# Corner sums of a bilinear gather: from wide SBUF multiplies to a PSUM accumulator, tap by tap, with new planner costs

## The chip, the cores and the metric

One NeuronCore of a Trainium2 chip runs the whole program. The metric is device time in microseconds of one execution, as the median of several; lower is better. The engines named below are PE (TensorE, matrix multiplies), DVE (VectorE), ACT (ScalarE), POOL (GpSimd) and SP (SyncE, which issues most DMAs). Each runs its own instructions in the order in which they were issued, and they wait for each other on semaphores.

## The reference, cut to what matters

Four layers are applied to each of four samples of shape 96 x 128 x 128: a two-direction selective scan (layer 0), a convolution mixed with Fourier transforms (layer 1), a modulated deformable convolution (layer 2), and a cosine transform with a 16-state scan (layer 3). Each is a residual branch behind a group normalisation. The change is in layer 2. Its core:

```python
offset = _conv(x, offset_w, offset_b)
mask = jax.nn.sigmoid(_conv(x, mask_w, mask_b))
for k in range(K * K):
    i, j = (k // K, k % K)
    py = base_y[None, :, None] + i * DIL + offset[:, 2 * k]
    px = base_x[None, None, :] + j * DIL + offset[:, 2 * k + 1]
    # v00, v01, v10, v11: the pixels around (py, px), zero outside
    samp = ((1 - wy_) * (1 - wx_) * v00 + (1 - wy_) * wx_ * v01
            + wy_ * (1 - wx_) * v10 + wy_ * wx_ * v11) * mask[:, k][:, None]
    out = out + jnp.einsum('bchw,oc->bohw', samp, weight[:, :, i, j])
return out + bias[None, :, None, None]
```

So each output pixel has nine taps, each tap four corners, and each corner 96 channels with one weight per pixel, tap and corner (the mask is multiplied into it beforehand).

## The kernel before, in words

**Stages.** For each sample there is a `front` (layer 0, layer 1, and the offsets, indices and corner weights of layer 2), a `back` (the gather of layer 2, and the head and first transform of layer 3), `layer3` (its scans) and an `inverse` transform. The program runs: the front of sample 0; then, for each sample b, one mixed stage with the back of b, the inverse of b-1 and the front of b+1, followed by layer3 of b; at the end the inverse of the last sample. The last mixed stage has no front.

**The planner.** In the prologue and in mixed stages, `Program` (from line 235) records every engine operation of two lanes, the back in lane 0, inverse and front in lane 1, and then issues them in an order that a list scheduler works out: it keeps a clock for each engine, gives each operation a duration from `cost` (line 351) and, between engines, `LATENCY` (line 243), and takes next, on the engine that can start soonest, the operation with the lowest key among those that can start within `LATENCY`. The key is an operation's place in its own lane, as a share of that lane's length, so both lanes advance in proportion. The order that comes out is fixed in the program; on the chip, each engine follows it whatever the real durations are. Since the recorder issues all operations, the profile shows line 65 for all of them, and tiles' names tell them apart. `layer3` uses another class, `Order`, with costs of its own.

**The gather** (`gather`, line 1270). A DRAM tensor `quad_d` holds, for each pixel, the 4 x 96 channels of a 2 x 2 neighbourhood. For each of 128 image rows and nine taps, POOL issues an indirect DMA that fetches 384 numbers for each of 128 pixels into `l_g` (three row buffers of 128 x 9 x 384). The loop at line 1344 runs over rows and taps: while row r is fetched, row r-1 is weighed, row r-2 is turned, and once in four rows a group of four is finished.

- `weigh` (line 1297), in three parts of three taps each: DVE multiplies 128 x 1152 numbers of `l_g` in place with their weights `l_v` (one weight spread over 96 channels), adds the second half of each tap's corners to the first (128 x 576), and adds the last two corners into `l_sm` (128 x 288). All three are on SBUF.
- `turn` (line 1311), in two parts: PE transposes `l_sm` in pieces of 128 columns into the PSUM tile `l_pt` (four in the first part, three in the second), and ACT copies them to `l_sT` on SBUF.
- `finish` (line 1328), in four parts: PE multiplies seven chunks of `l_sT`, for four rows at once, with the layer's weights into the PSUM tile `l_pc`; in the last part DVE adds bias and residual (`l_x`) and takes statistics of it.

The row buffer of `l_g` is free for a new row when `weigh` is done with it. `l_pt` and `l_pc` share one PSUM tag with two buffers. PSUM has eight banks; layer 0's own tags hold six of them (`a` three, `b` one, `c` two), the gather's two.

Of the kernel before, what the change touches and what calls it, by code (L numbers as in the profile page):

```python
# [45 lines left out]
def lanes(ap, n):  # L46

    return ap.unsqueeze(2).to_broadcast([ap.shape[0], ap.shape[1], n])
# [188 lines left out]
class Program:  # L237
# [4 lines left out]

    LATENCY = 0.12
    SPAN = (1.0, 1.0)
# [106 lines left out]
    def cost(self, engine, name, out, ins):  # L351

        if engine == "SP":
            v = next(v for v in [out, *ins] if isinstance(v, View) and v.tile.kind == "SBUF")
            return 0.1, 1.4e-5 * v.at[0].size * (v.rows[1] - v.rows[0])
        n = out.at[0].size
        if name == "indirect_dma_start":
            return 1.25, 0.68
        if engine == "PE":
            return (0.28 if name == "transpose" else 0.06 + 0.8 * n / CH), None  # L360
        if engine == "ACT":
            return 0.12 + 0.001 * n, None
        if engine == "POOL":
            return 0.1 + 0.0023 * n, None
        if name == "tensor_tensor_scan":
            return 0.1 + 0.0022 * n, None
        fast = name in ("tensor_copy", "tensor_scalar", "memset") and all(
            v.tile.kind == "SBUF" for v in [out, *ins]
        )
        return 0.09 + n / (1900 if fast else 960), None  # L370

# [122 lines left out]
class Net:  # L494
# [106 lines left out]
    def layer0(self, xin, T):  # L601
# [3 lines left out]
        with self.program.pool(name="l0w", bufs=1) as wp, self.program.pool(name="l0p", bufs=1, space=PSUM) as ps:  # L605
# [32 lines left out]
            for k in range(2):  # L638
                pw = ps.tile([128, CH], F32, name="l0_pw", tag="a", bufs=3)
                nc.tensor.matmul(out=pw[:C, :C], lhsT=xpd[:, k, :], rhs=dtT[:, k, :], start=True, stop=True)  # L640
                yield
                nc.vector.tensor_copy(wd[:, k, :], pw[:C, :C])
                for n in range(2):
                    nc.vector.tensor_copy(
                        wbc[:, 2 * k + n, :], xpT[:, k, R6 + n : R6 + n + 1].to_broadcast([C, C])
                    )
                yield
            scale, shift, _ = yield from self.group_norm(st0, ps, "a", 3)

            with self.program.pool(name="l0a", bufs=3) as wa:  # L650

                def block(i):
# [5 lines left out]
                    for g in range(4):  # L658
                        s = slice(BR * i * W + g * CH, BR * i * W + (g + 1) * CH)
                        pc = ps.tile([C, CH], F32, name="l0_pc", tag="a", bufs=3)  # L660
                        yield from self.conv9(pc, wc, xb, i, g)
# [15 lines left out]
            with self.program.pool(name="l0b", bufs=3) as wb:  # L677
                edges = [None, None]

                def scan(k, n):  # L680
# [60 lines left out]

                    pm = ps.tile([C, CH], F32, name="l0_pm", tag="a", bufs=3)
                    nc.tensor.matmul(out=pm, lhsT=center[:, 1, :], rhs=uc, start=True, stop=False)
# [7 lines left out]
                    yield  # L751
                    pv = ps.tile([C, CH], F32, name="cn_v", tag="a", bufs=3)
                    nc.tensor.matmul(out=pv, lhsT=self.cavg, rhs=sq, start=True, stop=True)
# [9 lines left out]
                    yield  # L763
                    po = ps.tile([C, CH], F32, name="l0_po", tag="a", bufs=3)
                    nc.tensor.matmul(out=po, lhsT=woT, rhs=ct, start=True, stop=True)
# [504 lines left out]
    def gather(self, T, wp, wb, ps):  # L1270
# [26 lines left out]
        def weigh(row, m):  # L1297
            g3 = gts[row][:, 3 * m : 3 * m + 3]
            if m == 0:
                sms[row] = wb.tile([128, 9, C], F32, name="l2_sm", tag="sm")  # L1300
            w4 = work[row // 4].w4[:, 36 * (row % 4) + 12 * m : 36 * (row % 4) + 12 * m + 12]
            gq = g3.rearrange("p k (q c) -> p (k q) c", c=C)
            nc.vector.tensor_tensor(gq, gq, lanes(w4, C), ALU.mult)
            nc.vector.tensor_tensor(
                g3[:, :, 0 : 2 * C], g3[:, :, 0 : 2 * C], g3[:, :, 2 * C : 4 * C], ALU.add
            )
            nc.vector.tensor_tensor(
                sms[row][:, 3 * m : 3 * m + 3], g3[:, :, 0:C], g3[:, :, C : 2 * C], ALU.add
            )

        def turn(row, m):
            w = work[row // 4]
            if row % 4 == 0 and m == 0:
                w.sT = wb.tile([128, KC, 4, W], F32, name="l2_sT", tag="sT")
            flat = sms[row].rearrange("p k c -> p (k c)")
            pt = ps.tile([128, 4, W], F32, name="l2_pt2", tag="t")
            k = 4 - m
            for j in range(k):
                at = (4 * m + j) * 128
                n = min(128, 9 * C - at)  # L1320
                nc.tensor.transpose(pt[:n, j, :], flat[:, at : at + n], self.ident)
            if m:
                nc.scalar.copy(w.sT[:, 4:6, row % 4, :], pt[:, 0:2])
                nc.scalar.copy(w.sT[:C, 6, row % 4, :], pt[:C, 2])
            else:
                nc.scalar.copy(w.sT[:, 0:4, row % 4, :], pt)

# [16 lines left out]
        for row in range(H + 3):  # L1344
            if row % 4 == 2 and row // 4 + 1 < H // 4:
                fetch(row // 4 + 1)
            for k in range(9):
                if row < H:
# [8 lines left out]
                    )  # L1357
                if k in (2, 4, 6) and 0 <= row - 1 < H:
                    weigh(row - 1, k // 2 - 1)
                if k in (1, 5) and 0 <= row - 2 < H:  # L1360
# [827 lines left out]
```

## Time and profile before

| | us |
|---|---|
| median of 7 runs | 18461.31 |
| lowest and highest of them | 18437.08, 18539.92 |
| the profiled execution | 18512.09 |
| its span | 18510.3 |
| DVE busy in the span | 13137.2 |
| POOL busy | 11661.8 |
| PE busy | 14440.1 |
| ACT busy | 8165.8 |

How to read the profile's lines: a group of instructions is named by its engine, its operation, what it writes and reads (`out<-in`, without buffer numbers), its shapes and its count; after the bar stand its busy time in us and the mean of one in ns, then the time for which the engine was idle just before such instructions, with what ended most of that. "issue" is idle time in which the engine waited for nothing that the profile shows, "remote" such that was ended by something the profile can't name. In a table of windows, each row is one stretch of the span, with every engine's busy time and count, then the clock granted to PE as a share of full speed, the DMA engines' share and GB/s. In a timeline a row is one or more instructions that follow each other, with start, length, and in brackets the engine's idle time before it.

### The profile page before, as it was taken

To read this page: it belongs to the slowest core of one execution; us is meant where nothing else is said; L and a number is where in the kernel's file an instruction comes from. 1 tells how busy PE (TensorE), PEld (TensorE's weight loads), DVE (VectorE), ACT (ScalarE), POOL (GpSimd) and SP (SyncE) were. 2 spreads that over 40 slices of the span, in tenths; PEclk is the share of its full clock that TensorE was granted. 3 is DMA by queue.
4 is the path that set the end of the run, shared out by engine and by line. 5 is a ranking of instruction groups with operands and counts; after the bars stand their busy time and mean duration, and the time that the engine had idled before them with its cause. 6 is when DMAs were issued, how large, how long until landed. Compare 5 with 4: busy or idle time off the path is not lost. (4 is left out here: it accounts for less than half of the span.)

```text
span 18510.3 us, 150202 instructions
## 1 busy us (share of the span) xinstructions
PE 14440.1 (78%) x41152; PEld 6545.3 (35%) x41152; DVE 13137.2 (71%) x17010; ACT 8165.8 (44%) x15519; POOL 11661.8 (63%) x9556
## 2 busy tenths in 40 slices
PE   7896877888988787888999587787899733248988
PEld 2363323543333322633333332454333311113334
DVE  1625586568998577667999658666899755557997
ACT  2612252126776143215777235213777500016776
POOL 0103686536887587553888668562788766656887
PEclk9897887989999888888999788798999955569999
DMA  3525557550001657553000555665000244440001
GB/s 82 159 78 160 166 163 210 162 171 27 9 7 43 180 163 208 161 163 108 9 7 8 150 159 164 201 172 171 11 7 9 70 143 139 137 124 23 9 7 48
DMA packets 1189374, 1939.48 MB, mean 105 GB/s; under 512 B 191985, under 2 KB 711601, under 8 KB 1169457
## 3 DMA queue, kind: packets, MB, share of 16 engines
q1 hardware_dynamic: 893616, 1023.60, 19.0%
q0 software_dynamic: 294912, 906.26, 17.0%
q8 instruction: 329, 5.39, 0.1%
q14 instruction: 517, 4.23, 0.1%
HBM read 1473.67 MB, written 455.61 MB: 104 GB/s over the span
## 5 line engine op out<-in xcount | busy, mean ns | idle before, releaser
L65 POOL DMA_INDIRECT l_g<-quad_d,l_i x4608 | 5450.5, 1183 | 3768.5 <-DVE l_sm L65 1443.8
L65 POOL TENSOR_TENSOR l_hc<-l_h,l_cs 128x512 f32<-128x512 f32 x3072 | 3854.6, 1274 | 848.3 <-PE l_py L65 264.4
L65 DVE TENSOR_TENSOR_SCAN l_h<-l_dA,l_carry,l_dB 128x512 f32<-128x512 f32 x3072 | 3916.3, 1275 | 166.4 <-ACT l_carry L65 74.5
L65 DVE TENSOR_TENSOR l_g<-l_g,l_v 128x1152 f32<-128x1152 f32 x1536 | 2085.2, 1358 | 911.0 <-DMA l_g<-quad_d,l_i 822.3
L65 ACT ACTIVATE l_dA<-l_dl,l_al 128x512 f32<-128x512 f32 x3072 | 2183.0, 722 | 802.4 <-DVE l_h L65 801.6
L65 ACT COPY l_sT<-l_pt 128x512 f32<-128x512 f32 (+2 forms) x1536 | 575.6, 407 | 4198.0 <-PE l_pt L65 2314.2
L65 PE MATMUL l_pt<-ident,l_sm 128*128 128x128 f32 (+1 forms) x3584 | 884.2, 340 | 1950.6 <-issue 726.2
L65 PE MATMUL l_py<-l_hc,ident 128*128 128x512 f32 x4608 | 2389.6, 608 | 18.4 <-POOL l_hc L65 10.1
L65 DVE TENSOR_TENSOR l_dB<-l_du,l_pB 128x512 f32<-128x512 f32 x3072 | 2135.8, 695 | 319.7 <-POOL l_du L65 26.7
L65 PE MATMUL l_pB<-l_bc,pick 128*128 128x512 f32 x3072 | 1781.2, 580 | 554.5 <-DVE l_dB L65 521.8
L65 ACT COPY l_cs<-l_pC 128x512 f32<-128x512 f32 x3072 | 1785.2, 581 | 630.0 <-PE l_pC L65 540.4
L65 PE MATMUL l_pC<-l_bc,pick 128*128 128x512 f32 x3072 | 1549.7, 504 | 118.8 <-ACT l_cs L65 108.4
L65 PEld LDWEIGHTS l_pt<-ident,l_sm 128*128 128x128 f32 (+1 forms) x3584 | 510.5, 167 | 2773.2 <-issue 1840.8
L65 PEld LDWEIGHTS l_pB<-l_bc,pick 128*128 128x128 f32 x3072 | 582.3, 190 | 2198.7 <-DVE l_dB L65 2104.6
L65 DVE TENSOR_TENSOR l_g<-l_g 128x576 f32<-128x576 f32 x1536 | 1165.2, 759 | 36.1
L65 PE MATMUL l_p<-rows,l_c 96*96 96x508 f32 (+2 forms) x2304 | 1076.0, 610 | 33.8 <-DMA rows<-cat_d 17.2
L65 PE MATMUL l_pc<-rows,l_wc 96*96 96x508 f32 (+2 forms) x2304 | 1083.6, 608 | 10.6 <-issue 5.6
L65 PE MATMUL l_pu<-l_xq,l_wc 96*64 96x512 f32 (+1 forms) x2048 | 1078.6, 616 | 13.6 <-ACT l_xq L65 13.6
L65 PE MATMUL l_pc<-l_sT,l_wk 128*96 128x512 f32 (+1 forms) x1792 | 986.7, 670 | 62.6 <-ACT l_sT L65 36.6
L65 PEld LDWEIGHTS l_py<-l_hc,ident 128*128 128x128 f32 x4608 | 882.7, 193 | 379.2 <-issue 173.6
L65 POOL TENSOR_TENSOR l_hc<-l_hc 128x512 f32<-128x512 f32 x768 | 977.9, 1273 | 55.2
L65 DVE TENSOR_TENSOR l_sm<-l_g 128x288 f32<-128x288 f32 x1536 | 699.7, 472 | 353.4 <-remote 221.2
(252 smaller groups left out, 20861.9 us busy)
## 6 DMA issues: line engine op xcount, KB each, us to landing
quad_d<-l_qt SPq DMA_DIRECT2D x124, 768.0 KB
x<-l_x SPq DMA_DIRECT2D x384, 192.0 KB
l_g<-quad_d,l_i POOLq DMA_INDIRECT x4608
mix<-l_mx SPq DMA_DIRECT2D x256, 256.0 KB
sp_in<-mix SPq DMA_DIRECT2D x256, 256.0 KB
l_uc<-u_d SPq DMA_DIRECT2D x256, 192.0 KB
l_x<-x SPq DMA_DIRECT2D x256, 192.0 KB
l_xs<-x SPq DMA_DIRECT2D x116, 256.0 KB
```

The costliest lines, as they stand in the source:

```text
L65: ins = op(*args, **kw).ins
```

## The change

It has three parts.

1. `weigh` runs in two parts instead of three, over taps 0 to 4 and 5 to 8, when row r's taps 2 and 5 are fetched (2, 4 and 6 before). Each part takes a PSUM tile `l_acc` of 128 x 5 x 96 (one bank, one buffer). For each tap ACT writes the first corner times its weight into `l_acc`, with the weight as a scale by pointer; then DVE adds the second and third corner to it, one multiply-add of 128 x 96 for each tap and corner, and the fourth corner's multiply-add writes to `l_sm`. `l_g` is only read.
2. `turn` transposes three pieces in its first part and four in its second (four and three before), since the first part of `weigh` makes five taps, which is 480 columns.
3. To make room for `l_acc`, layer 0's PSUM tag `a` has two buffers instead of three. The planner's costs are changed: `LATENCY` 0.2 instead of 0.12, and other durations by kind of operation.

```diff
-    LATENCY = 0.12
+    LATENCY = 0.2
...
         if engine == "PE":
-            return (0.28 if name == "transpose" else 0.06 + 0.8 * n / CH), None
+            return (0.2 if name == "transpose" else 0.06 + 0.83 * n / CH), None
         if engine == "ACT":
-            return 0.12 + 0.001 * n, None
+            return 0.12 + (0.0009 if name == "copy" else 0.0011) * n, None
         if engine == "POOL":
+            return 0.2 + 0.0023 * n, None
+        if name == "tensor_tensor_scan":
             return 0.1 + 0.0023 * n, None
-        if name == "tensor_tensor_scan":
-            return 0.1 + 0.0022 * n, None
...
-        return 0.09 + n / (1900 if fast else 960), None
+        return (0.1 if n < 200 else 0.14) + n / (1900 if fast else 960), None
...
-                        pc = ps.tile([C, CH], F32, name="l0_pc", tag="a", bufs=3)
+                        pc = ps.tile([C, CH], F32, name="l0_pc", tag="a", bufs=2)
...
         def weigh(row, m):
-            g3 = gts[row][:, 3 * m : 3 * m + 3]
             if m == 0:
                 sms[row] = wb.tile([128, 9, C], F32, name="l2_sm", tag="sm")
-            w4 = work[row // 4].w4[:, 36 * (row % 4) + 12 * m : 36 * (row % 4) + 12 * m + 12]
-            gq = g3.rearrange("p k (q c) -> p (k q) c", c=C)
-            nc.vector.tensor_tensor(gq, gq, lanes(w4, C), ALU.mult)
-            nc.vector.tensor_tensor(
-                g3[:, :, 0 : 2 * C], g3[:, :, 0 : 2 * C], g3[:, :, 2 * C : 4 * C], ALU.add
-            )
-            nc.vector.tensor_tensor(
-                sms[row][:, 3 * m : 3 * m + 3], g3[:, :, 0:C], g3[:, :, C : 2 * C], ALU.add
-            )
+            acc = ps.tile([128, 5, C], F32, name="l2_acc", tag="acc", bufs=1)
+            w4 = work[row // 4].w4
+            taps = range(5 * m, 5 + 4 * m)
+            for q in range(4):
+                for k in taps:
+                    at = 36 * (row % 4) + 4 * k + q
+                    g, w = gts[row][:, k, q * C : (q + 1) * C], w4[:, at : at + 1]
+                    a_ = acc[:, k - 5 * m, :]
+                    if q == 0:
+                        nc.scalar.activation(a_, g, AF.Copy, scale=w)
+                    else:
+                        o = sms[row][:, k, :] if q == 3 else a_
+                        nc.vector.scalar_tensor_tensor(o, g, w, a_, ALU.mult, ALU.add)
...
-            k = 4 - m
+            k = 3 + m
             for j in range(k):
-                at = (4 * m + j) * 128
+                at = (3 * m + j) * 128
...
             if m:
-                nc.scalar.copy(w.sT[:, 4:6, row % 4, :], pt[:, 0:2])
-                nc.scalar.copy(w.sT[:C, 6, row % 4, :], pt[:C, 2])
+                nc.scalar.copy(w.sT[:, 3:6, row % 4, :], pt[:, 0:3])
+                nc.scalar.copy(w.sT[:C, 6, row % 4, :], pt[:C, 3])
             else:
-                nc.scalar.copy(w.sT[:, 0:4, row % 4, :], pt)
+                nc.scalar.copy(w.sT[:, 0:3, row % 4, :], pt[:, 0:3])
...
-                if k in (2, 4, 6) and 0 <= row - 1 < H:
-                    weigh(row - 1, k // 2 - 1)
+                if k in (2, 5) and 0 <= row - 1 < H:
+                    weigh(row - 1, k // 5)
```

The other four PSUM tiles of layer 0's tag `a`, and the call of the group normalisation that uses it, change from three to two buffers in the same way.

More of the change, by code (lines that the diff above doesn't have):

```diff
@@ L638, in layer0 @@
             for k in range(2):
-                pw = ps.tile([128, CH], F32, name="l0_pw", tag="a", bufs=3)
+                pw = ps.tile([128, CH], F32, name="l0_pw", tag="a", bufs=2)
                 nc.tensor.matmul(out=pw[:C, :C], lhsT=xpd[:, k, :], rhs=dtT[:, k, :], start=True, stop=True)
@@ L647, in layer0 @@
                 yield
-            scale, shift, _ = yield from self.group_norm(st0, ps, "a", 3)
+            scale, shift, _ = yield from self.group_norm(st0, ps, "a", 2)
             with self.program.pool(name="l0a", bufs=3) as wa:
@@ L739, in scan @@
                     yield
-                    pm = ps.tile([C, CH], F32, name="l0_pm", tag="a", bufs=3)
+                    pm = ps.tile([C, CH], F32, name="l0_pm", tag="a", bufs=2)
                     nc.tensor.matmul(out=pm, lhsT=center[:, 1, :], rhs=uc, start=True, stop=False)
@@ L751, in scan @@
                     yield
-                    pv = ps.tile([C, CH], F32, name="cn_v", tag="a", bufs=3)
+                    pv = ps.tile([C, CH], F32, name="cn_v", tag="a", bufs=2)
                     nc.tensor.matmul(out=pv, lhsT=self.cavg, rhs=sq, start=True, stop=True)
@@ L763, in scan @@
                     yield
-                    po = ps.tile([C, CH], F32, name="l0_po", tag="a", bufs=3)
+                    po = ps.tile([C, CH], F32, name="l0_po", tag="a", bufs=2)
                     nc.tensor.matmul(out=po, lhsT=woT, rhs=ct, start=True, stop=True)
```

## The prediction

> **What bounds the kernel now.** I read the page first, then the busy times stage by stage, then one stretch of the stage in which the gather runs without a front beside it, then the groups of single stages.
>
> ```profile
> span 18510.3 us, 150202 instructions
> ...
> L65 POOL DMA_INDIRECT l_g<-quad_d,l_i x4608 | 5450.5, 1183 | 3768.5 <-DVE l_sm L65 1443.8
> ...
> L65 DVE TENSOR_TENSOR l_g<-l_g,l_v 128x1152 f32<-128x1152 f32 x1536 | 2085.2, 1358 | 911.0 <-DMA l_g<-quad_d,l_i 822.3
> ```
>
> ```profile
> core 0: us, PE busy (x) PEld busy (x) DVE busy (x) ACT busy (x) POOL busy (x), PEclk, DMA share, GB/s
> 0.00:1530.00 1530.00, 1304.00 (x3998) 628.51 (x3999) 557.26 (x920) 490.13 (x991) 91.64 (x68) 0.94 0.38 109
> ...
> 5950.00:8570.00 2620.00, 2072.84 (x6547) 1007.77 (x6546) 1714.46 (x2498) 744.10 (x1600) 1557.09 (x1248) 0.85 0.61 178
> ...
> 14700.00:16700.00 2000.00, 684.87 (x2206) 344.65 (x2204) 1130.49 (x1403) 210.61 (x499) 1218.12 (x1185) 0.61 0.49 142
> ```
>
> The span falls into a front alone (1530 us), three mixed stages (2760, 2620 and 2680 us: gather of one sample beside the front of the next), a last gather stage with only the short inverse beside it (2000 us), and four layer3 stages (1660, 1760, 1690 and 1811 us), which the change doesn't touch. In a mixed stage no engine is full: PE 2073/2620 = 79%, DVE 65%, POOL 59%. What one is late for changes within the stage: in 6500 to 7000 us (the scans of layer 0) POOL is busy 405 us and idle 54 us more between gathers while PE's clock is down to 0.84; in 7500 to 8000 us PE is busy 444 of 500. The last gather stage is DVE's: 814 gathers in 15000 to 16250 us are 90.4 rows, so a row takes 13.8 us, though POOL can issue one in 9 x 1.25 = 11.3 us. There the instructions stand so:
>
> ```profile
> start us, us, engine line op out<-in xcount [idle before <-releaser]
> ...
> 15501.64 0.76 DVE L65 TENSOR_TENSOR l_g<-l_g 128x576 f32<-128x576 f32 x1
> 15502.43 0.46 DVE L65 TENSOR_TENSOR l_sm<-l_g 128x288 f32<-128x288 f32 x1
> 15502.73 0.98 POOL L65 DMA_INDIRECT l_g<-quad_d,l_i  x1 [0.30 <-issue]
> 15502.81 1.35 DVE L65 TENSOR_TENSOR l_g<-l_g,l_v 128x1152 f32<-128x1152 f32 x1
> 15503.01 0.47 PEld L65 LDWEIGHTS l_pt<-ident,l_sm 128*128 128x128 f32 x3 [2.32 <-issue]
> 15503.04 0.87 PE L65 MATMUL l_pt<-ident,l_sm 128*128 128x128 f32 x3 [1.95 <-DVE l_sm L65]
> 15503.94 0.53 ACT L65 COPY l_sT<-l_pt 128x256 f32<-128x256 f32 x2 [2.24 <-issue]
> 15504.02 0.96 POOL L65 DMA_INDIRECT l_g<-quad_d,l_i  x1 [0.30 <-issue]
> 15504.19 0.76 DVE L65 TENSOR_TENSOR l_g<-l_g 128x576 f32<-128x576 f32 x1
> ```
>
> To be seen here: a Vector instruction that needs the one before it starts 0.03 us after its end (15502.81 + 1.35 to 15504.19); one that doesn't starts 0.08 us before that end (15502.43 + 0.46 to 15502.81). Vector goes on with the next taps while PE and ACT turn the last ones.
>
> **Vector's part, step by step.** Removed per row: three times (1358 + 759 + 472 ns) = 7.8 us. Added: 27 multiply-adds of 96 elements. Their price comes from these rows of the last gather stage and of the whole:
>
> ```profile
> L65 DVE SCALAR_TENSOR_TENSOR l_x<-l_pc,l_bk,l_x 96x512 f32<-96x512 f32 x32 | 23.9, 746 | 445.1 <-remote 181.0 <-PE l_pc L65 132.6 <-issue 131.5
> ```
>
> This is the same operation with a scalar by pointer and one PSUM operand, 746 ns at 512 elements. 1152 and 576 elements give a slope of (1358 - 759)/576 = 1.04 ns, so 96 elements cost 746 - 416 x 1.04 = 313 ns. The other end is the multiply-add on SBUF alone that makes l_idx, 301 ns at 144: 301 - 48 x 1.04 = 251 ns. No row writes PSUM from Vector; I take 313, whose operands are nearest. In the built order all of the second and third products, and the first of the fourth ones, wait for the instruction just before them, although it is another tap; only the other fourth products are free. So a batch of n taps takes 2n x (d + 0.03) + (n - 1)(d - 0.08) + d: at 0.313 this is 4.7 us for five taps and 3.8 for four, 8.4 a row (+0.6 over today); at 0.251 it is 6.8 (-1.0).
>
> The Trainium skill speaks against the cut: "VectorE: DVE Perf Modes", "Rules for kernel authors", advises for chained operations to keep their count low rather than to fuse. Its formula (N + 151)/0.96 GHz gives 257 ns for 96 elements, an estimate by which a row would be 6.9 us; the row of 746 ns lies 55 ns above what the same formula gives for 512, so the trace's price is dearer.
>
> **ACT's part and the hand-over.** Nine products of 96 elements a row. Dearest: l_dA (scale by pointer, SBUF to SBUF) 722 ns at 512, with the slope of ACT's copies (586 - 372)/256 = 0.84 ns: 722 - 416 x 0.84 = 373 ns. Cheapest: the copy of 96x128, 264 ns, less 32 x 0.84: 237. In the built order each waits for the one before (+0.03), and the first multiply-add waits for the last product of its batch. There is one accumulator buffer, so the first product waits until Vector has finished the batch before. ACT and Vector therefore take turns: neither end of today's chain has this wait. In the last stage ACT also has the copies of the turned sums between the second and third product, and these wait for PE's transposes of the batch just finished: 1.05 us from l_sm's end (15502.89) to the copy (15503.94), the copies 0.37 + 0.26 or about 0.5, then three or two more products. With 0.40 a product: 1.05 + 0.63 + 1.2 = 2.9 and 1.05 + 0.5 + 0.8 = 2.35, so 5.2 us a row in which Vector stands; with 0.27 it is 4.6.
>
> **The sum by stage.** Last gather stage, dear end: 8.4 + 5.2 + four hand-overs of 0.1 = 14.0 us, plus l_x and its statistics (746 + 690 ns every four rows, 0.4), plus today's idle time before l_x unchanged (445.1/128 = 3.5): 17.9 a row, against 13.8 today, x 128 = +530 us. Cheap end: 6.8 + 4.6 + 0.4 + 0.4 + 1 (the wait before l_x cut to that) = 13.2, x 128 = -80 us. I take the middle, +220. Mixed stages: Vector's own work +0.6 x 128 = +80 us. In the built order half of a stage's 256 batches follow the one before on Vector with nothing between; 128 x about 1.8 us of products (five of 0.40 or four) = 230 us is the most that it then stands. Both shown: +310. Against it: POOL's gather takes 1234 ns in 5950 to 8570 us, 1018 in the last stage, and 0.95 us where Vector is idle, so what replaces the two-operand multiplies can return up to (1234 - 1018) ns x 1152 = 250 us. Since PE, not Vector, is nearest to full, I take a third of the loss and a fifth of the gain: +50 each, +150 for three. ACT has the room for 9 x 0.4 x 128 = 460 us a stage (744 of 2620 busy). Front alone: layer 0's PSUM tag loses one of three buffers. What hides this is that a group of nine tap matmuls of about 0.6 us (5.4 us) covers a 0.68 us ACT read; in the 300 us of scans, with three chained tiles per step, the cover is thin: between 0 and 30 us, taken as 15, with the new costs' reordering (below nothing is possible too: -30). Sum: 220 + 150 + 15 = +385 on 18,510 (the execution ran 18,512 us, the span nearly all of it); the median of the runs is 18,461, 50 below, so I forecast 18,850 us. Its own range: 18,600 to 19,300.
>
> The Trainium skill bears on the gain, too: "SBUF — State Buffer" states that Vector and GpSimd share a port pair that a Vector instruction with two SBUF inputs holds for its whole length. The 0.95 against 1234 ns agrees; by the rule alone all of the gather's stretching by the weighing would go.
>
> **The rivals.** *POOL set free (ends faster).* The new multiply-adds have one SBUF tensor instead of two. If POOL sets the pace of the scan phase (405 + 54 of 500 us there, gathers of 1480 ns), then the gathers' shortening shows: half of 250 us less 30 for Vector = about -95 in each mixed stage, and the cheap end -80 in the last: 18,461 - 365 = about 18,100. For it: DVE's waits for the gather's landing, 287 us in one mixed stage. Against: Vector's and ACT's turns are longer than the span saved. It decides once a chained multiply-add is below about 0.27 us. *Turns everywhere.* The dear ends hold in all stages: 3 x 310 + 530 = +1460, 19,920 us. For it: ACT's in-order queue blocks front evacuations behind a product that waits for Vector, with only two PSUM buffers. Against: 906 us of Vector's time in such a stage is idle now. *Nothing moves:* l_x's wait and PE set both kinds of stage, and the new work fills idle time: 18,461.
>
> **How the numbers follow.** Forecast 0.46, turns everywhere 0.12, nothing 0.08, POOL free 0.34. A measurement of this kernel tells 0.3% (55 us) from no change: slower 0.58, same 0.08, faster 0.34. The range must reach into POOL's case and part of the turns': 18,200 to 19,450 leaves about 1 in 10 at each end.
>
> **What would show it.** Right: l_acc multiply-adds near 313 ns, rows of the last gather stage at 15 us or more, Vector's idle time before l_acc ended by ACT, the last stage longer than 2000 us by some 220, the layer3 stages as before. Wrong: multiply-adds at 250 ns or less; gathers near 1000 ns in the mixed stages and these below 2600 us; the front alone moving by over 50 us.

## The result, and the profile after

The changed kernel took 18603.59 us (median of 14 runs, 18564.81 to 18622.49) beside 18523.83 us of the kernel before (35 runs, 18429.07 to 18582.09): a ratio of 1.0052, 95% interval 1.0038 to 1.0067. It is slower by half a per cent, by 80 us; 18,850 us had been forecast, 389 more than the 18,461 us of the first seven runs of the kernel before.

From the page of the changed kernel, the span and the groups of the new weighing (busy time, mean ns of one, then the idle time before them and what ended most of it):

```profile
span 18584.4 us, 171591 instructions
...
L65 POOL DMA_INDIRECT l_g<-quad_d,l_i x4608 | 4499.0, 976 | 4705.6 <-ACT l_acc L65 2156.9
L65 DVE SCALAR_TENSOR_TENSOR l_acc<-l_g,l_v,l_acc 128x96 f32<-128x96 f32 x9216 | 2965.6, 322 | 1989.2 <-ACT l_acc L65 1272.0
...
L65 ACT ACTIVATE l_acc<-l_g,l_v 128x96 f32<-128x96 f32 x4608 | 1583.1, 344 | 3302.4 <-DVE l_sm L65 2132.8
...
L65 DVE SCALAR_TENSOR_TENSOR l_sm<-l_g,l_v,l_acc 128x96 f32<-128x96 f32 x4608 | 1141.3, 308 | 286.4 <-PE l_pt L65 98.2
```

POOL's gathers fell from 1183 to 976 ns. The price is in the two waits: Vector stood 1272 us for ACT's products, and ACT stood 2133 us for the end of Vector's batch. Each of the two waits for the other over one accumulator.

The span is cut at the scans of layer3, which last about 1660 us in each of its four stages in both traces. What lies between, in us (the first stretch is the front alone with the first mixed stage):

| stretch | before | after | difference |
|---|---|---|---|
| start to first layer3 scan | 4273 | 4269 | -4 |
| second mixed stage | 2714 | 2768 | +54 |
| third mixed stage | 2710 | 2754 | +44 |
| last gather stage | 2091 | 2076 | -15 |

The sum, +79 us, is near the difference of the medians (79.8 us) and of the two spans (74 us). The second and third mixed stages lost about the 50 us each that had been forecast. The first stretch, for which +65 stood in the sum (15 for the front, 50 for its mixed stage), did not lose: up to the first gather it became 28 us shorter (1653 to 1625 us), and behind it 24 us longer (2620 to 2644). The last gather stage, for which +220 had been forecast, did not lose at all.

One turn in the last gather stage of the changed kernel, from its timeline (start, length, in brackets the idle time of the engine):

```profile
15501.38 0.99 DVE L65 SCALAR_TENSOR_TENSOR l_sm<-l_g,l_v,l_acc 128x96 f32<-128x96 f32 x4
15501.84 1.09 PE L65 MATMUL l_pt<-ident,l_sm 128*128 128x128 f32 x4 [4.80 <-DVE l_sm L65]
15502.41 0.72 ACT L65 ACTIVATE l_acc<-l_g,l_v 128x96 f32<-128x96 f32 x2 [3.93 <-DMA l_g<-quad_d,l_i]
...
15503.07 0.62 ACT L65 COPY l_sT<-l_pt 128x384 f32<-128x384 f32 x2
15503.59 1.10 ACT L65 ACTIVATE l_acc<-l_g,l_v 128x96 f32<-128x96 f32 x3
15504.72 3.55 DVE L65 SCALAR_TENSOR_TENSOR l_acc<-l_g,l_v,l_acc 128x96 f32<-128x96 f32 x10 [2.35 <-ACT l_acc L65]
15508.38 1.21 DVE L65 SCALAR_TENSOR_TENSOR l_sm<-l_g,l_v,l_acc 128x96 f32<-128x96 f32 x5
```

Vector ends a batch at 15502.37. ACT then makes two products, copies the turned sums, makes three more, and only when the fifth has ended (15504.69) does Vector begin: 2.35 us of standing before a batch of five taps, and 1.82 before one of four. A row is 8.6 us of Vector's work and 4.2 us of this. In the same stage, the groups of 15000 to 16250 us have this line:

```profile
L65 DVE SCALAR_TENSOR_TENSOR l_x<-l_pc,l_bk,l_x 96x512 f32<-96x512 f32 x23 | 17.2, 747 | 76.4 <-PE l_pc L65 58.1 <-remote 10.9 <-issue 7.4
```

Before `l_x` Vector waited 76.4/23 = 3.3 us for a group of four rows, against 445.1/32 = 13.9 in the kernel before. That is 2.7 us a row less. A second wait of the kernel before is gone as well, the one before `l_sm`. Here is its group in 14700 to 16700 us before, then in 15000 to 16250 us after:

```profile
L65 DVE TENSOR_TENSOR l_sm<-l_g 128x288 f32<-128x288 f32 x384 | 175.9, 458 | 294.9 <-remote 210.5 <-issue 67.9
```

```profile
L65 DVE SCALAR_TENSOR_TENSOR l_sm<-l_g,l_v,l_acc 128x96 f32<-128x96 f32 x833 | 203.9, 310 | 11.1 <-DVE l_acc L65 1.4
```

That is 294.9/128 = 2.3 us a row against 0.1. Together the two waits are 4.9 us a row shorter. That covers the 4.2 us of the turns and what Vector's own work grew by, so the stage did not lose.

### The profile page after: what moved, and what is told of

It reads as the page before. It is cut to its first block, busy times and chain, and to the rows that moved or that the text cites. A ratio compares the mean times of both kernels' runs of the same rounds, so it can differ in the third digit from the quotient of the medians.

```text
span 18584.4 us, 171591 instructions
## 1 busy us (share of the span) xinstructions
PE 14454.7 (78%) x41152; PEld 6583.7 (35%) x41152; DVE 13408.2 (72%) x26226; ACT 9537.5 (51%) x20127; POOL 10677.0 (57%) x9556
## 5 line engine op out<-in xcount | busy, mean ns | idle before, releaser
L65 POOL DMA_INDIRECT l_g<-quad_d,l_i x4608 | 4499.0, 976 | 4705.6 <-ACT l_acc L65 2156.9
L65 DVE SCALAR_TENSOR_TENSOR l_acc<-l_g,l_v,l_acc 128x96 f32<-128x96 f32 x9216 | 2965.6, 322 | 1989.2 <-ACT l_acc L65 1272.0
L65 ACT ACTIVATE l_acc<-l_g,l_v 128x96 f32<-128x96 f32 x4608 | 1583.1, 344 | 3302.4 <-DVE l_sm L65 2132.8
L65 DVE SCALAR_TENSOR_TENSOR l_sm<-l_g,l_v,l_acc 128x96 f32<-128x96 f32 x4608 | 1141.3, 308 | 286.4 <-PE l_pt L65 98.2
L65 PE MATMUL l_pc<-rows,l_wc 96*96 96x508 f32 (+2 forms) x2304 | 1080.1, 611 | 13.8 <-DVE rows L65 12.2
L65 PE MATMUL l_p<-rows,l_c 96*96 96x508 f32 (+2 forms) x2304 | 1054.8, 601 | 27.1 <-DMA rows<-cat_d 13.9
L65 PEld LDWEIGHTS l_pC<-l_bc,pick 128*128 128x128 f32 x3072 | 583.4, 190 | 994.5 <-ACT l_cs L65 671.8
```

The costliest lines, as they stand in the source:

```text
L65: ins = op(*args, **kw).ins
```

## The experiments

Three theories were put to the test. T1: the turns of ACT and Vector cost what POOL's shorter gathers give back. T2: the planner's new order made the difference. T3: layer 0's third PSUM buffer did.

The runs came in five groups, each on another chip, with the kernel before beside them. The chips turned out to be of two kinds, called A (kernel before at 18247 to 18282 us) and B (18498 to 18506 us; the comparison above, at 18524, counts as B). No chip was met twice, so it isn't shown that the chip itself, and not something else that changed from one group to the next, makes the kind. All runs at a glance; the stretches are those of the table above:

| run | kind | median, us | ratio to before, interval | first | 2nd mixed | 3rd mixed | last |
|---|---|---|---|---|---|---|---|
| e2, before with two buffers in layer 0 | A | 18270.40 | 0.9999, 0.9990 to 1.0008 | 4207 | 2677 | 2691 | 1977 |
| e1, before with new costs | A | 18177.62 | 0.9956, 0.9942 to 0.9969 | 4162 | 2643 | 2655 | 1974 |
| e16, the same again | A | 18155.75 | 0.9951, 0.9937 to 0.9964 | 4157 | 2649 | 2652 | 1975 |
| e12, changed kernel | A | 18094.58 | 0.9898, 0.9883 to 0.9913 | 4141 | 2605 | 2599 | 2018 |
| e0, changed kernel | B | 18500.82 | 1.0026, 1.0007 to 1.0044 | 4252 | 2736 | 2728 | 2055 |
| e3, changed, old costs | A | 18346.21 | 1.0039, 1.0025 to 1.0053 | 4218 | 2688 | 2692 | 2024 |
| e13, changed, old LATENCY | B | 18699.27 | 1.0110, 1.0081 to 1.0139 | 4310 | 2797 | 2803 | 2089 |
| e6, second accumulator, last stage | B | 18507.50 | 1.0014, 0.9994 to 1.0034 | 4253 | 2735 | 2738 | 2068 |
| e14, the same again | B | 18619.97 | 1.0073, 1.0046 to 1.0100 | 4267 | 2762 | 2770 | 2096 |
| e10, and products a batch ahead | A | 17917.87 | 0.9798, 0.9785 to 0.9812 | 4142 | 2606 | 2610 | 1841 |
| e9, product on Vector | A | 18032.27 | 0.9860, 0.9845 to 0.9875 | 4127 | 2617 | 2622 | 1944 |
| e17, the same again | A | 18034.37 | 0.9883, 0.9868 to 0.9898 | 4132 | 2614 | 2619 | 1947 |
| e4, first product in SBUF | A | 17546.81 | 0.9606, 0.9593 to 0.9619 | 4019 | 2527 | 2534 | 1740 |
| e11, the same again | A | 17547.99 | 0.9599, 0.9586 to 0.9613 | 4024 | 2516 | 2540 | 1741 |
| e15, the same again | B | 18948.58 | 1.0247, 1.0217 to 1.0276 | 4314 | 2845 | 2831 | 2218 |
| e8, that with old costs | B | 20074.78 | 1.0868, 1.0834 to 1.0902 | 4726 | 3240 | 3211 | 2191 |
| e7, whole accumulator in SBUF | B | 18623.52 | 1.0083, 1.0053 to 1.0113 | 4283 | 2769 | 2781 | 2066 |
| e5, before, third buffer, last stage | B | 18459.82 | 0.9991, 0.9966 to 1.0015 | 4261 | 2727 | 2737 | 1987 |

### Layer 0's buffers alone, and the order alone

```diff
 e2_tag_only, from the kernel before:
-                        pc = ps.tile([C, CH], F32, name="l0_pc", tag="a", bufs=3)
+                        pc = ps.tile([C, CH], F32, name="l0_pc", tag="a", bufs=2)
...
 e1_costs_only, from the kernel before (cost as in the change):
-    LATENCY = 0.12
+    LATENCY = 0.2
...
 e3_old_costs, from the changed kernel (cost as before):
-    LATENCY = 0.2
+    LATENCY = 0.12
```

> The kernel before with layer 0's PSUM tag at two buffers instead of three, nothing else. T1: 0.999 to 1.002, front alone within 15 us. T2: the same. T3: 1.003 to 1.006, with the front alone and each mixed stage longer by 20 to 40 us, all of it in layer 0's part.

> The kernel before with nothing but the planner's new LATENCY and durations. Theories: (T1) the turns of ACT and Vector over the one accumulator cost the three mixed stages what the shorter gathers give back, and the new order does little: ratio to the kernel before 0.998 to 1.002, each stage within 20 us of before. (T2) the order made the difference: then this run carries it, 1.004 to 1.006, the mixed stages +40 to +55 us each. (T3) layer 0's two PSUM buffers instead of three made it: ratio 1.000 here.

> The changed kernel with the planner's old LATENCY and durations. T1: 1.003 to 1.008 against the kernel before, as the changed kernel, since the turns are still there. T2: outside that: 1.000 (the new order costs 80 us) or 1.012 and more (the new order saves what the turns cost, 130 us or more, most of it in the mixed stages). T3: 1.005.

> The kernel before with the new LATENCY and durations alone. On a chip where the kernel before takes about 18270 us: 0.995 to 0.997, as in the first such run. Where it takes about 18500 us: 0.994 to 0.998 if the order is worth the same there, so that the new weighing costs 0.6 to 1.0% there; 0.999 to 1.003 if late hand-overs undo what the order gains.

The two buffers cost nothing (0.9999, on kind A): T3 falls there, and on chips of kind A this run can stand for the kernel before, of which no trace was taken there. The new order alone is a gain, which no theory had: 0.9956, and 0.9951 in the repeat, which met kind A again. 34 and 36 us of it lie in the second and third mixed stage. With the new weighing the old costs gave 1.0039, within what T1 expected; but this doesn't speak for T1, since the changed kernel itself is 0.9898 on such a chip (below). So the order is worth 0.4% with the old weighing and 1.4% with the new one, the latter from runs on two chips of one kind.

### The same program on chips of two kinds

> The changed kernel itself, beside the others, with a trace of its own. With the old durations it was 1.0039 of the kernel before, and the new durations alone were worth 0.9956 on the kernel before. If the two add up (T2: the order counts in both kernels alike): 0.999 to 1.001. If the turns of ACT and Vector set the pace whatever the order (T1): 1.003 to 1.006. The last gather stage is the test of the wait before l_x: where the kernel before has no idle time of 445 us before l_x, T1 expects the changed kernel's last stage to be longer than the other's by 30 to 60 us instead of shorter by 15.

> The changed kernel beside it on the same chip. All theories: 1.000 to 1.006 against the kernel before. What tells is its last stretch of gathers beside that of the run before it in this list: T1 1700 to 1760 us, some 260 to 300 us more.

On kind B the changed kernel was 1.0026, on kind A 0.9898, outside what anyone had expected: the sign of the change depends on the chip. On kind A it gains 72 and 92 us in the mixed stages and 66 in the first stretch, and loses 41 in the last stage (against e2). The 41 us are within the 30 to 60 that were expected where the kernel before has no long wait before `l_x`. What is different can be read from Vector's waits in one mixed stage (engine, line, releaser: us in total, times, longest). The changed kernel on the chip of the recorded comparison, 5952 to 8281 us:

```profile
DVE l_acc L65 <- ACT l_acc L65: 310.5, 161, 25.1
DVE l_acc L65 <- issue: 64.9, 33, 7.6
...
DVE l_sm L65 <- remote: 30.9, 6, 9.0
```

And on a chip of kind A, 5825 to 7993 us:

```profile
DVE l_acc L65 <- ACT l_acc L65: 343.0, 202, 5.6
DVE sp_ta L65 <- PE sp_a L65: 58.5, 28, 5.0
DVE rows L65 <- DMA rows<-in_x: 51.5, 3, 31.6
```

The wait for ACT's products is there in both, 311 and 343 us. Waits that nothing in the profile ends ("issue", "remote") are there only in the first: over all of Vector's instructions in this stage they come to 138 us, and to none on kind A; for ACT to 334 us and 1, for PE to 84 us and none. The longest wait for ACT is 25.1 us there and 5.6 on kind A, though the order of the instructions is the same.

### The last gather stage: buffer, or place in ACT's queue

```diff
 e6_acc2_last, e14_acc2_last_again, from the changed kernel (self.last: the last sample's back):
-            acc = ps.tile([128, 5, C], F32, name="l2_acc", tag="acc", bufs=1)
+            acc = ps.tile([128, 5, C], F32, name="l2_acc", tag="acc", bufs=2 if self.last else 1)
...
 e10_ahead_last, besides: first() makes the products of a batch, adds() its multiply-adds
+                if self.last:
+                    if k == 2 and 0 <= row - 1 < H:
+                        if row == 1:
+                            first(0, 0)
+                        first(row - 1, 1)
+                        adds(row - 1, 0)
+                    if k == 5 and 0 <= row - 1 < H:
+                        if row < H:
+                            first(row, 0)
+                        adds(row - 1, 1)
```

> The changed kernel with a second accumulator buffer in PSUM, in the last gather stage alone, where banks are free; the mixed stages stay as they are. T1 (the turn over one buffer is the cost there): the last stretch of gathers falls from about 1700 to 1760 us to 1440 to 1520 us, the row from 13.3 to 13.7 us to POOL's 11.3 to 11.8; ratio to the kernel before 0.985 to 0.992. Rival: ACT's products writing PSUM in a chain, or their wait behind the copies of the turned sums, are the cost, not the buffer: then the stretch stays above 1650 us.

> The changed kernel with two accumulator buffers in the last gather stage, as in the run with the second buffer alone, and there also with ACT's products of a batch recorded one batch ahead of Vector's multiply-adds. A second buffer alone left the stage at 1751 us. T1 (what Vector waits for is the last product of its own batch, which stands behind the copies of the turned sums): 1440 to 1520 us. Rival (PE's late hand-overs or the wait before l_x hold the stage): above 1650 us.

> The changed kernel with a second accumulator buffer in the last gather stage alone. With products recorded a batch ahead as well, the stretch of gathers was 1530 us on a chip where the changed kernel has 1700. If the second buffer is what counts: 1530 to 1580 us, ratio within 0.003 of that run's 0.980. If Vector's wait for the last product of its own batch is what counts, which stands behind the copies of the turned sums: 1650 to 1760 us, ratio within 0.003 of the changed kernel's (0.990 on such a chip, 1.003 to 1.005 on the other kind).

On one chip of kind B, the stretch of gathers was 1736 us in the changed kernel and 1751 us with the second buffer: the buffer alone brings nothing there. On a chip of kind A it was 1700 us in the changed kernel and 1530 us with the products a batch ahead, a little over T1's 1520. (e14 again found no gain from the buffer: 1780 us, more than either theory expected, on another chip of kind B without the changed kernel beside it. On kind A the buffer alone never ran.) So what Vector waits for, as the timeline above has it, is the last product of its own batch. It stands in ACT's queue behind the copies, which wait for PE's transposes of the batch that Vector has just finished; a second buffer lets the first two products run early and leaves the other three where they were.

### No hand-over from ACT

```diff
 e9_product_dve, e17_product_dve_again, from the changed kernel:
-                        nc.scalar.activation(a_, g, AF.Copy, scale=w)
+                        nc.vector.tensor_scalar_mul(a_, g, w)
```

> The changed kernel with the first product on Vector as well (a multiply by a pointer scalar into the PSUM accumulator), so that ACT has no part in the weighing and no hand-over is left; Vector has 9 x 128 more instructions of about 0.3 us in each stage, 345 us. T1: the last stretch of gathers 1540 to 1640 us (36 x 0.33 + 0.4 us a row), shorter than the changed kernel's although Vector works more; mixed stages 20 us shorter to 40 longer; ratio 0.985 to 1.000. Rival (what Vector has to do sets the mixed stages, not the hand-over): the mixed stages longer by 150 us and more each, ratio above 1.015.

> The changed kernel with the first product on Vector, so that no hand-over from ACT to Vector is left in the weighing. On a chip where the kernel before takes about 18270 us: 0.985 to 0.988, as in the first such run. Where it takes about 18500 us: 0.985 to 0.996 if the changed kernel's loss there (from 0.990 to 1.003 to 1.005) comes from ACT's hand-overs to Vector; 1.000 to 1.008 if it comes from PE's ends being seen late, which this kernel has as well.

0.9860 and 0.9883, both on kind A. The groups of the last stage (14600 to 15850 us) show the wait for ACT gone, and 29.6 + 62.0 us of idle time left before 2635 instructions on the accumulator:

```profile
L65 DVE SCALAR_TENSOR_TENSOR l_acc<-l_g,l_v,l_acc 128x96 f32<-128x96 f32 x1756 | 567.0, 323 | 62.0
L65 DVE TENSOR_SCALAR l_acc<-l_g,l_v 128x96 f32<-128x96 f32 x879 | 281.3, 320 | 29.6
```

9 x 0.32 = 2.9 us a row more on Vector replaced 4.2 us of standing: the last stage went from 2018 to 1944 us, the mixed stages from 2605 and 2599 to 2617 and 2622, all as T1 expected. Vector had the room for some 370 us more in them (9 x 128 x 0.32); the rival that its work sets these stages falls, on kind A. The repeat met kind A again, so what happens on kind B stays open.

### The first product in SBUF

```diff
 e4_first_sbuf, e11_first_sbuf_again, e15_first_sbuf_third, from the changed kernel:
+            first = wb.tile([128, 5, C], F32, name="l2_first", tag="first", bufs=3)
...
-                        nc.scalar.activation(a_, g, AF.Copy, scale=w)
+                        nc.scalar.activation(f_, g, AF.Copy, scale=w)
...
-                        nc.vector.scalar_tensor_tensor(o, g, w, a_, ALU.mult, ALU.add)
+                        nc.vector.scalar_tensor_tensor(o, g, w, f_ if q == 1 else a_, ALU.mult, ALU.add)
```

> The changed kernel with ACT's first products written to an SBUF tile of three buffers; Vector's first multiply-add reads it there and writes the PSUM accumulator, which only Vector then touches. The turns are gone; the price is 9 multiply-adds a row with two SBUF inputs. T1: the last gather stage, 1758 us of gathers with rows of 13.7 us, comes down to what Vector needs (8.4 + 0.4 us) or POOL's 9 x 1.25 = 11.3 us a row, 1450 to 1550 us; the mixed stages lose 30 to 100 us each; ratio to the kernel before 0.978 to 0.990. T2 and T3: the mixed stages stay at 2754 to 2768 us, and only the last stage is shorter: 0.988 to 0.995. If the two-SBUF reads stretch the gathers again, gathers in the mixed stages rise from 976 to 1050 ns or more, and it ends at 1.000.

> The run with the first product in SBUF once more, since the calls so far ran on chips on which the kernel before takes 18268 and 18506 us, and it is to be compared with the others on one chip. T1 (the hand-over from ACT to Vector is the cost, and the gain of POOL's shorter gathers shows once it is gone): 0.955 to 0.970 against the kernel before on this chip too, last stretch of gathers 1440 to 1480 us. T2 (the gain was the chip's, or an order that happened to suit it): above 0.985 here.

> The run with the first product in SBUF beside these, to see whether its gain holds on a chip where the kernel before takes 18500 us: T1 without any share of the late hand-overs 0.955 to 0.965 on either kind of chip; if late hand-overs take as much of it as of the changed kernel (some 400 us more than on the other kind, where the kernel before loses 240): 0.965 to 0.975.

On kind A this is the best version of all, 0.9606 and 0.9599, and 547 us below the changed kernel on the same chip: 277 in the last stage, 89 and 59 in the mixed stages, 117 in the first stretch. Vector's wait for ACT in a mixed stage (5707 to 7800 us) is down from 343 to 73 us:

```profile
DVE l_acc L65 <- ACT l_first L65: 72.6, 55, 5.0
```

In the SBUF tile Vector's first multiply-add of a tap follows that tap's product:

```profile
14338.59 1.44 ACT L65 ACTIVATE l_first<-l_g,l_v 128x96 f32<-128x96 f32 x5
...
14339.00 0.33 DVE L65 SCALAR_TENSOR_TENSOR l_acc<-l_g,l_v,l_first 128x96 f32<-128x96 f32 x1 [2.99 <-ACT l_first L65]
```

ACT's five products run until 14340.03, and Vector begins 1.03 us before. Over the PSUM tile it followed the last product of the batch. The edit changes two things at once, this hand-over and the number of buffers (three instead of one); that a second PSUM buffer alone brought nothing speaks for the hand-over, but that was on kind B. In the last stage a row takes 1443/128 = 11.3 us, nine gathers at 1.25: POOL's own pace.

On kind B the same program took 1.0247, which no theory had allowed for; only e8 was slower. The granted clock doesn't tell the two apart: in 1000 us of the last stage it is 0.58 on kind A (14300 to 15300 us) and 0.57 on kind B (15300 to 16300 us). Here is the end of a group of four rows in the last stage, first on kind A, then on kind B:

```profile
14337.42 0.60 PE L65 MATMUL l_pt<-ident,l_sm 128*128 128x128 f32 x4
14337.85 1.88 PE L65 MATMUL l_pc<-l_sT,l_wk 128*96 128x512 f32 x4
14338.05 0.64 ACT L65 COPY l_sT<-l_pt 128x384 f32<-128x384 f32 x2 [5.33 <-PE l_pt L65]
...
14339.77 0.75 DVE L65 SCALAR_TENSOR_TENSOR l_x<-l_pc,l_bk,l_x 96x512 f32<-96x512 f32 x1 [0.45 <-PE l_pc L65]
```

```profile
15343.62 0.60 PE L65 MATMUL l_pt<-ident,l_sm 128*128 128x128 f32 x4
15344.06 1.88 PE L65 MATMUL l_pc<-l_sT,l_wk 128*96 128x512 f32 x4
15350.49 0.64 ACT L65 COPY l_sT<-l_pt 128x384 f32<-128x384 f32 x2 [10.98 <-remote]
...
15358.19 0.75 DVE L65 SCALAR_TENSOR_TENSOR l_x<-l_pc,l_bk,l_x 96x512 f32<-96x512 f32 x1 [6.43 <-remote]
```

On kind A the copy starts 0.03 us after the transposes' end and `l_x` 0.04 us after that of the products `l_pc`. On kind B the records of PE look the same, and the copy comes 6.27 and `l_x` 12.25 us after them. Over the whole program, ACT's idle time before these copies, first on kind A, then on kind B:

```profile
L65 ACT COPY l_sT<-l_pt 128x384 f32<-128x384 f32 (+1 forms) x1536 | 574.7, 404 | 2173.9 <-PE l_pt L65 2172.7
```

```profile
L65 ACT COPY l_sT<-l_pt 128x384 f32<-128x384 f32 (+1 forms) x1536 | 575.9, 405 | 3331.7 <-PE l_pt L65 2030.7 <-remote 697.8 <-issue 343.4
```

1041 us ended by nothing that the profile can name, against next to none. Since PE's ends are modelled, this may be PE that is later than its records, or its signal that is late; the traces don't tell.

### The same with the old costs, the accumulator in SBUF, and a third buffer before

```diff
 e8_first_sbuf_old_costs: e4_first_sbuf with LATENCY and cost as before
 e13_old_latency, from the changed kernel:
-    LATENCY = 0.2
+    LATENCY = 0.12
...
 e7_acc_sbuf, from the changed kernel (layer 0's tag a: three buffers again):
-            acc = ps.tile([128, 5, C], F32, name="l2_acc", tag="acc", bufs=1)
+            acc = wb.tile([128, 5, C], F32, name="l2_acc", tag="acc", bufs=2)
...
 e5_t3_last, from the kernel before:
-            "l2q", 2, PSUM
+            "l2q", 3 if self.last else 2, PSUM
```

> The run with the first product in SBUF, with the planner's old LATENCY and durations. T2 (the new order is worth 0.4% on its own, as on the kernel before): 0.964 to 0.967 against 0.9606 with the new ones. T1 (what it gained is the turn alone): 0.959 to 0.963. If the order made that gain: above 0.975.

> The changed kernel with the planner's old LATENCY of 0.12 and the new durations. On chips where the kernel before takes about 18270 us, the changed kernel was 0.990 of it, and 1.004 with both old. If the durations make that difference: 0.988 to 0.993 there. If LATENCY makes it: 1.000 to 1.006. On a chip like that of 18506 us: 1.002 to 1.006 by the first, 1.012 and more by the second.

> The changed kernel with the accumulator in SBUF (two buffers), and layer 0's PSUM tag back at three: no turns, but all 27 multiply-adds of a row read two SBUF inputs instead of 9 in the run with the first product alone in SBUF. If the two-SBUF reads are what stretched POOL's gathers in the kernel before: gathers of 1100 to 1300 ns in the mixed stages, against 992 ns with the first product alone in SBUF, and these stages at 2600 to 2690 us, ratio 0.980 to 1.000. If it was only that the wide multiplies held Vector long: gathers at 1000 ns and a ratio of 0.960 as with the first product in SBUF.

> The kernel before with three instead of two PSUM buffers for the turned sums and the group's product in the last gather stage alone. On a chip where Vector waits long before l_x (445 us there): if the wait comes from the two buffers shared with the transposes, the stretch of gathers falls from 1774 to 1650 to 1690 us; if PE's ends are seen late there whatever the buffers, it stays at 1740 to 1790. On a chip without that wait both expect 1670 to 1690 us, as in the run with layer 0's two buffers, and nothing is told apart.

e8 took 1.0868 on kind B, where the new costs gave 1.0247 on another such chip; what had been expected of it started from kind A's 0.9606 and can't be read from it. In its trace there are, in each mixed stage, 646 matmuls of the gather in a row with none of the front between them (at most 49 with the new costs, in e4 and e15), and the windows show what that does (us; busy time and count of PE, PEld, DVE, ACT and POOL, then the granted clock, the DMA share and GB/s):

```profile
2750.00:3500.00 750.00, 223.66 (x609) 104.42 (x607) 455.39 (x1478) 197.13 (x651) 448.39 (x472) 0.59 0.48 136
3750.00:4250.00 500.00, 486.41 (x2019) 313.20 (x2016) 156.90 (x281) 105.91 (x279) 16.71 (x12) 0.96 0.36 107
```

For 750 us PE is busy for 30%, while the gather runs alone; then the rest of the front runs alone. A plan made with wrong durations can undo a good cut of the work.

e13 came out at 1.0110 on kind B, just below what was expected if LATENCY carries the order's share. The changed kernel was not beside it on that chip, but e14 was, which has the changed kernel's order up to the last stage: against e14, e13 is 79 us slower, its first stretch by 43 us and its mixed stages by 35 and 33. So the old LATENCY alone costs something there; what the durations cost was not tried alone.

e7 shows gathers of 1007 ns in a mixed stage (1159.99 us for 1152), although all 27 multiply-adds of a row read two SBUF tensors, so the expected 1100 to 1300 ns didn't come. It is slower than the changed kernel on the same chip all the same (18623.52 against 18500.82 us); no line tells where that is from, beyond `l_sm` at 325 instead of 308 ns.

e5 leaves the question open. In its trace Vector's wait before `l_x` is nearly gone (38.6 us for 31 groups) and the stretch of gathers is 1692 us. But its median doesn't differ from that of the kernel before: the interval allows a gain of 63 us at most (0.9966), and the theory of the buffers asked for 84 to 124. So either the buffers aren't the cause, or the kernel before mostly hadn't the wait on that chip; its own times on such chips lie from 18396 to 18573 us, and the trace of e5 may be of an execution that hadn't the wait anyway.

## Why the prediction was right or wrong

**Prices: right.** Multiply-adds were put at 313 ns and took 322 into PSUM and 308 into SBUF; their chain cost 0.035 us against 0.03; a product 0.36 us with its chain against 0.40. The formula cited from the Trainium skill stands in "VectorE: DVE Perf Modes" under "The TRN2 errata — SBUF-src ops pay a fixed extra latency per instruction", for a plain fp32 `tensor_tensor` add of 512 and 2048 elements; the estimate of 257 ns for 96 was too low here, and the measurement decides.

**Layer 0's third buffer: right.** +15 us between -30 and +30 was forecast; alone, on kind A, the whole kernel was 0.9999, and in the change the stretch up to the first gather fell by 28 us.

**POOL's gathers: right in size.** 1234 ns in a mixed stage went to 986 (1135.88 us for 1152); 248 ns came back where 216 had been put down as the most.

**Three mixed stages at +50 each: near for two of them on the recorded chip (+54 and +44; the first grew by 24), and by luck, since the reasoning wasn't right.** It weighed "a third of the loss and a fifth of the gain". On kind A, Vector stood 343 us in a mixed stage before `l_acc`, more than the 230 us put down as the most; and still these stages became 72 and 92 us shorter, as the rival *POOL set free* had it. Its condition, a chained multiply-add below about 0.27 us, was wrong: at 0.36 us the gain showed. Of it, 34 and 36 us are the order's, which the sum had at most at -30 in all. What turned the gain into a loss on kind B had no term in the sum: the same program's mixed stages are 163 and 155 us longer on the recorded chip than on kind A, the kernel before's only 37 and 19. That the changed kernel suffers more because more of its hand-overs have no slack is argued from these numbers, not shown.

**The last gather stage at +220: the step that failed.** It is 235 of the 310 us by which the whole forecast was too high (+389 against +80). The +220 was the middle between a cheap end of 13.2 us a row and a dear one of 17.9, that is 15.5. Two terms of the dear end were mis-sized. The turns were put at 5.2 us a row and four hand-overs of 0.1; they took 4.2 with the hand-overs, because PE begins to transpose single pieces before the batch's last `l_sm` has ended. And "today's idle time before `l_x` unchanged (445.1/128 = 3.5)" fell to 76.4/92 = 0.8 us a row. Together that is 4.1 us a row less than the dear end of 17.9, and 13.7 was measured (a stretch of gathers of 1758 us by 128). The sum took over that wait as a property of the kernel. The wait before `l_sm` (2.3 us a row), which also stood in the 13.8 us of the old row, the prediction didn't name; its sum for the new row left it out, and it did go. Neither wait comes with the work itself: on kind A the kernel before, for which e2 stands, has neither (20 us before `l_sm` in its whole last stage). Here are e2's groups in the last stage (14800 to 16050 us):

```profile
L65 DVE TENSOR_TENSOR l_g<-l_g,l_v 128x1152 f32<-128x1152 f32 x285 | 386.9, 1358 | 448.8 <-DMA l_g<-quad_d,l_i 448.6
...
L65 DVE SCALAR_TENSOR_TENSOR l_x<-l_pc,l_bk,l_x 96x512 f32<-96x512 f32 x23 | 17.1, 745 | 10.3 <-PE l_pc L65 10.2
```

There Vector waits 448.6 us for gathers to land and 10.3 before `l_x`: the stage isn't DVE's, as the prediction read it, but POOL's, whose gathers stretch under the wide multiplies (a stretch of 1682 us, 13.1 a row). The changed kernel replaced that by its turns (1700 us, 13.3 a row), and the stage lost 41 us, not 220. On the recorded chip the turns took the place of the waits before `l_x` and `l_sm`, and the stage lost nothing. That these waits differ from one execution of the kernel before to the next is argued, from its spread (144 to 177 us from the lowest to the highest on kind B, 39 to 58 on kind A); only one such execution on kind B was traced. Why the changed kernel hasn't got them there stays open.

**The signs named ahead.** Multiply-adds near 313 ns, Vector's idle time before `l_acc` ended by ACT, layer3 as before: seen. Rows of 15 us and a longer last stage: not seen. Gathers near 1000 ns together with mixed stages below 2600 us had been named as a sign against the forecast; the gathers came, and the mixed stages grew on that chip all the same. The front moved by less than 50 us.

**Still open:** what makes the hand-overs late on kind B, and how the +0.5% there divides between the order and the weighing; the run meant for that (e16) met kind A.

## What to carry to other kernels

A wait in one profiled execution whose releaser is "remote" or "issue" should not enter a sum as a constant: take the stage's next bound as well, and forecast from both. When two engines fill and empty one buffer, look at what stands between the products in the feeding engine's queue before adding a buffer: a second buffer brought nothing (on kind B), a batch of lead or a hand-over by tap brought 177 and 277 us in the last stage (on kind A). After a change of the cut, give a static planner the measured durations, and measure on more than one chip where a version has little slack in its hand-overs.

## What the runs showed of the hardware

Two kinds of chips. The version with the first product in SBUF took 17548 us on one chip and 18949 on another, 8% apart; the kernel before 1.5% (18247 to 18524), the changed kernel 2.2 to 2.8% (18095 against 18501 and 18604). Each chip was met once.

Short multiply-adds with two SBUF inputs hardly stretch POOL's gathers. With 27 of some 0.33 us a row (e7) a gather took 995 ns, with wide multiplies of 1.36 us 1183 (the kernel before) and 1223 (e2), with PSUM accumulation 979 (e0, on e7's chip). The Trainium skill ("SBUF — State Buffer", "SBUF: two separate sides") says that a Vector instruction with two SBUF inputs takes the port pair that it shares with GpSimd for its whole length, against a GpSimd instruction that reads SBUF; the gather has its indices `l_i` there. That fits the wide multiplies; for the short ones the loss measured here is 16 ns a gather. The wide ones also work in place and are another operation, so that it is the length that counts isn't shown.

Vector's 128x96 instructions lie close together: a multiply-add took 322 ns with its sum in PSUM, 308 from PSUM into SBUF, 325 to 329 on SBUF alone (e7) and 345 with both tensors in SBUF and the result in PSUM (e11); a product into PSUM took 320 (e9). ACT's product took 344 ns into PSUM and 367 into SBUF.
